# Where the decay exponents of a Mamba-2 scan are formed: matrix products before, broadcast rows with a Relu per head after

## The chip, the cores and the metric

The kernel runs on one core of a Trainium2 chip. The metric is device time in microseconds (us), the median of three runs of the whole kernel. Engines are named as in the profile: PE (TensorE, with its weight loads as PEld), DVE (VectorE), ACT (ScalarE), POOL (GpSimd), SP (the queue that issues most DMAs).

## The reference, cut to what matters

The input is 16 sequences of 512 tokens with 256 features. Each is normalized, goes through a Mamba-2 block with 8 heads, is normalized and added, and goes through a feed-forward block with ternary weights. Around the change, this is computed for every sequence:

```python
zxbcdt = x @ in_proj_w.T                        # z, x|B|C, dt
xBC = silu(conv4(xBC) + conv_b)
dt = softplus(dt + dt_bias)
dA = exp(dt * A)                                # A = -exp(A_log), one per head
S = dA_t * S + xdt_t[..., None] * B_t           # the scan over tokens
y_t = einsum('bhpn,bn->bhp', S, C_t)
```

Both kernels run the scan in four chunks of 128 tokens. Inside a chunk the output needs, for every head h, source token s and target token t, the factor exp(cum[t,h] - cum[s,h]) for t at or after s, where cum is the running sum of dt*A in the chunk. These factors fill a tile `mt` of 128 x (8 heads x 128) per chunk.

## The kernel before, in words

The order of work on PE, DVE, ACT and POOL is written out by hand: generator functions (stages) emit instructions, and `interleave` steps each stage between two fractions of a stretch. Each engine then runs its own instructions strictly in that order. Only SP's order is left to the scheduler. After a start with sequences 0 and 1, a loop of 14 turns does two stretches per turn, for three sequences at once:

- First stretch: input projections, convolution and gate of the next sequence (`stage_a`, blocks "b" and "z"), output projection and norms of the previous one (`stage_c1`), and on POOL the products of C with decays (`stage_e`, L533).
- Second stretch: feed-forward of the previous sequence (`stage_c2`: eight hidden blocks with Gelu, L756 and L762, then four output blocks, L790), the scan of the current one (`stage_b2`), and softplus, running sums and exponentials of the next (`stage_a2`, `stage_b0`, `stage_b1`).

The names that matter below:

- A convolution block is a product `pm` (PE, L323), a scaled copy to `cv` (ACT, L328), three multiply-adds on `cv` (DVE, L330) and a Silu (ACT, L335) that runs one block later (`lag=1`). The sixth block's Silu, which gives C, is emitted by `stage_a6` in the next first stretch.
- `stage_c1` makes `po` (PE, L710, one per chunk, in a pool of two PSUM banks) and `att` (DVE, L716), which needs the factor `rms` from a power on POOL (L585); then norm statistics whose power is on POOL (L258, `rs_c`), the second stream (L696), and a normalized copy (ACT, L282) that PE turns (L736) and DVE splits (`rests`, L740).
- `stage_a2` is softplus on 128x32: a Silu (L416), a reciprocal, and a series of eight coefficients `ATANH`, then `a = dt*A` (L465).
- `sums_of` makes three small products of `a` into `pd` (L477, L478), copies them to `sums` (DVE) and `cum` (ACT, L483), splits `cum` into three bf16 parts (L486 to L489), and brings these by DRAM (`away`, L491) into row groups of `lhs_e` and `rhs_e` (L492, L495).
- `stage_b1`: for each chunk two bf16 products `pe` of `lhs_e` with `rhs_e` (PE, L549, 128x512 each). These two constant tiles also hold ones and a mask, so that `pe` is already cum[t]-cum[s], or a large negative number. ACT takes exp of each (L553).
- `stage_b2`, per chunk: transposes `px` (L593), `xdt` (DVE, L595), `pg` with C.B (L599) and a turned B (L600), its masking (L602), a copy `bT` (DVE, L606), `xend` (POOL, L608), `mt = min(mt,1)*pg` (DVE, L611), the chunk's state `pst` (PE, L628), the decayed former state (POOL, L633) and their sum (DVE, L636), the output `py` (PE, L644 and L651) and `y` (DVE, L657).

The Exp functions need another ACT table than the Silus and the Gelus, so that each turn has three table loads: before the Gelus, before the Exps (L507), and before the Silus (L335).

Of the kernel before, what the change touches and what calls it, by code (L numbers as in the profile page):

```python
# [52 lines left out]
ATANH = [1.0 / k for k in (17, 15, 13, 11, 9, 7, 5, 3)]  # L54
# [3 lines left out]
def mamba_ffn_kernel(  # L58
# [25 lines left out]
    big = ctx.enter_context(tc.tile_pool(name="big", bufs=4))  # L84
# [31 lines left out]

    rhs_e = const.tile([P, NC, NH, P], BF16)
    lhs_e = const.tile([P, NC, P], BF16)  # L120

    def exponent_constants():

        nc.gpsimd.affine_select(
            out=rhs_e[:, 0], in_=rhs_e[:, 0], compare_op=ALU.is_ge, fill=-1e30, base=126,
            pattern=[[0, NH], [1, P]], channel_multiplier=-2,
        )
        yield 1.0
        for j in range(3):
            nc.gpsimd.affine_select(  # L130
                out=rhs_e[:, 0], in_=rhs_e[:, 0], compare_op=ALU.not_equal, fill=-1.0, base=-j,
                pattern=[[-3, NH], [0, P]], channel_multiplier=1,
            )
            yield 1.0

        for j in range(2):
            nc.gpsimd.affine_select(
                out=lhs_e, in_=lhs_e, compare_op=ALU.not_equal, fill=1.0, base=126 - j,
                pattern=[[0, NC], [1, P]], channel_multiplier=-2,
            )  # L140
            yield 1.0
        nc.gpsimd.memset(lhs_e[0:27], 1.0)
        for c in range(1, NC):
            nc.scalar.copy(rhs_e[:, c], rhs_e[:, 0])
            yield 1.0

# [293 lines left out]
    def stage_a2(b):  # L440


        W = NC * NH
        dt, neg, sil = seqs[b]["dt"], seqs[b].pop("neg"), seqs[b].pop("sil")
        df = dt.rearrange("p c h -> p (c h)")
        z = small.tile([P, W], F32, tag="sp_z", name=f"sp_z_{b}", bufs=1)
        nc.vector.scalar_tensor_tensor(z, neg, 2.0, sil, ALU.mult, ALU.subtract)
        nc.vector.reciprocal(z, z)
        nc.vector.tensor_mul(z, z, sil)
        e = small.tile([P, W], F32, tag="sp_e", name=f"sp_e_{b}", bufs=1)  # L450
        nc.vector.tensor_mul(e, z, z)
# [6 lines left out]
        for k in ATANH[4:]:  # L458
# [8 lines left out]
        sums_of(b, a)  # L467
        yield 0.3

    def sums_of(b, a):  # L470


        W = NC * NH
        af = a.rearrange("p c h -> p (c h)")
        pd = ps_tr.tile([P, 512], F32, tag="tr", name=f"pd_{b}")
        for i, tri in enumerate((after, ones)):
            nc.tensor.matmul(pd[:, i * W : (i + 1) * W], tri, af, start=True, stop=True)  # L477
        nc.tensor.matmul(pd[0:W, 2 * W : 2 * W + P], af, incl, start=True, stop=True)  # L478
        sums = small.tile([P, 2, W], F32, tag="sums", name=f"sums_{b}")
        nc.vector.tensor_copy(sums.rearrange("p i w -> p (i w)"), pd[:, 0 : 2 * W])  # L480
# [4 lines left out]
        rest = small.tile([W, P], F32, tag="cr", name=f"cr_{b}", bufs=1)  # L485
        nc.vector.tensor_copy(cp[:, 0, :], pc)  # L486
        nc.vector.tensor_sub(rest, pc, cp[:, 0, :])
        nc.vector.tensor_copy(cp[:, 1, :], rest)
        nc.vector.tensor_sub(cp[:, 2, :], rest, cp[:, 1, :])  # L489
        away = dram.tile([NC, NH, 3, P], BF16, tag="away", name=f"away_{b}")  # L490
        nc.sync.dma_start(away.rearrange("c h j t -> (c h) j t"), cp)  # L491
        nc.sync.dma_start(  # L492
            lhs_e[0:24], away.rearrange("c h j t -> (h j) c t")
        )
        nc.sync.dma_start(  # L495
            rhs_e[24:27].rearrange("j c h t -> j (c h) t"),
            away.rearrange("c h j t -> j (c h) t"),
        )
        seqs[b].update(sums=sums, cum=cum)


    def stage_b0(b):


        s = seqs[b]
        s["dec"] = small.tile([P, 2, NC, NH], F32, tag="dec", name=f"dec_{b}")
        nc.scalar.activation(  # L507
            s["dec"].rearrange("p i c h -> p (i c h)"), s["sums"].rearrange("p i w -> p (i w)"),
            AF.Exp,
        )  # L510
        cum = s.pop("cum")
        nc.scalar.activation(cum, cum, AF.Exp)
        s["way"] = dram.tile([NC * NH, P], F32, tag="way", name=f"way_{b}")
        nc.sync.dma_start(s["way"], cum)
        yield 0.1
# [24 lines left out]
    def stage_b1(b, lo, hi):  # L540

        mts = seqs[b].setdefault("mts", [])
        for c in range(lo, hi):
            n = f"{b}_{c}"
            mt = big.tile([P, NH, P], F32, tag="mt", name=f"mt_{n}")
            for q in range(2):
                hs = slice(4 * q, 4 * q + 4)
                pe = ps_a.tile([P, 512], F32, tag="a", name=f"pe_{n}_{q}")
                nc.tensor.matmul(  # L549
                    pe, lhs_e[:, c, :], rhs_e[:, c, hs, :].rearrange("p h t -> p (h t)"),  # L550
                    start=True, stop=True,
                )
                nc.scalar.activation(mt[:, hs, :].rearrange("p h t -> p (h t)"), pe, AF.Exp)  # L553
                yield 0.25
            mts.append(mt)


    def stage_b2(b):
# [28 lines left out]
        def prepare(c):  # L587
# [23 lines left out]
            nc.vector.scalar_tensor_tensor(  # L611
                mts[c], mts[c], 1.0, cbt.unsqueeze(1).to_broadcast([P, NH, P]), ALU.min, ALU.mult
# [8 lines left out]
        for c in range(NC):  # L621
# [3 lines left out]
            if c < NC - 1:  # L625
# [16 lines left out]
            for j in range(NJ):  # L642
# [7 lines left out]
                for h in (2 * j, 2 * j + 1):  # L650
# [3 lines left out]
                    )  # L654
            y = sb.tile([P, NJ, P], F32, tag="yt", name=f"y_{n}")
# [181 lines left out]
    A0_WORK, T0_WORK, A_WORK, A2_WORK, B1_WORK, B2_WORK = 1.0, 0.9, 18.1, 1.0, 0.5, 14.9  # L837
# [15 lines left out]
    with tc.manual_schedule(engines=ordered):  # L853
        nc.vector.memset(rhs_e[:, 0], 0.0)
        nc.vector.memset(lhs_e, 0.0)
# [29 lines left out]
        for i in range(1, NB - 1):  # L885
# [17 lines left out]
            second.append((stage_a2(i + 1), A2_WORK, 0.15, 0.5))  # L903
# [5 lines left out]
            interleave(*second)  # L909
        run(stage_a6(NB - 1))  # L910
# [52 lines left out]
```

## Time and profile before

| | |
|---|---|
| median of three runs (lowest to highest) | 1172.53 us (1172.21 to 1173.19) |
| the profiled execution | 1170.62 us, its span 1168.9 us |
| busy: PE, DVE, ACT, POOL | 1110.5 (95%), 850.3 (73%), 568.5 (49%), 594.6 us (51%) |
| mean granted PE clock | 0.98 |
| one turn of the loop | 68.50 us (ACT's first L553 of two successive turns starts at 578.02 and 646.52 us) |
| L549, the exponents' products | 128 on PE, 47.0 us busy |
| L553, their exponentials | 128 on ACT, 73.5 us busy, mean 595 ns |

How to read the rows that follow. A row of groups gives line, engine, operation, tiles written and read, shapes and count, then busy time and the mean of one, then how long the engine had been idle just before, and what ended that. A row of the timeline gives start and length in us, and in brackets how long the engine sat idle before it and which instruction ended the wait. Matmuls overlap in the pipeline: a row says 0.38 us for one, and what one costs in a full stream is the distance between starts.

### The profile page before, as it was taken

Reading aid. Unit: us, or ns where it says so; the run is one execution under the profiler, and the core shown is the slowest. Engines: PE = TensorE matmul, PEld = TensorE weight load, DVE = VectorE, ACT = ScalarE, POOL = GpSimd, SP = SyncE. Lnnn points to the kernel's source line nnn. Section 1 sums busy time; section 2 is a strip of 40 time slices with the busy share of each in tenths; the row PEclk is TensorE's granted clock in tenths of the full one; section 3 lists DMA queues with packets and bytes.
Section 4 is the critical chain, followed back from the end, with each engine's and each line's share of the span. In section 5 each row is a group of like instructions: output and inputs, shape, how many; then the busy total and the mean of one; then the engine's idle time right before and its main releaser. Section 6 shows DMA issues by size and latency. Waiting matters only on the chain.

```text
span 1168.9 us, 16958 instructions
## 1 busy us (share of the span) xinstructions
PE 1110.5 (95%) x6164; PEld 726.3 (62%) x6164; DVE 850.3 (73%) x2211; ACT 568.5 (49%) x957; POOL 594.6 (51%) x706
## 2 busy tenths in 40 slices
PE   5778899999999999999999999999999999999797
PEld 2335476675757667575765757576575756657475
DVE  4587977768687776868777686977768697786552
ACT  4725545446453544646355464635546463553321
POOL 3453545455454645546454554645455464555743
PEclk9888999999999999999999999999999999999899
DMA  5101011020100102010020101002020100201000
GB/s 194 40 19 57 19 43 52 4 73 19 68 27 31 64 5 72 19 67 28 20 74 4 73 19 67 27 10 85 4 72 19 68 27 4 72 5 72 2 10 27
DMA packets 28627, 48.57 MB, mean 42 GB/s; under 512 B 6656, under 2 KB 25728, under 8 KB 26496
## 3 DMA queue, kind: packets, MB, share of 16 engines
q1 hardware_dynamic: 26992, 47.33, 11.9%
q8 instruction: 48, 0.79, 0.3%
q10 hardware_dynamic: 1552, 0.16, 0.1%
q14 instruction: 35, 0.29, 0.1%
HBM read 38.44 MB, written 9.04 MB: 41 GB/s over the span
## 4 chain that ended last, share of the span: by engine, by line
PE 82%; DVE 7%; POOL 6%; ACT 3%; DMA 1%; issue 1%; POOLq 0%; ACTq 0%
PE pf L790 20%; PE pm L323 13%; PE ph L756 12%; PE po L710 9%; PE pz L345 8%; PE py L644 5%; PE pst L628 3%; PE py L651 3%; POOL x3p L744 3%; PE pe L549 2%; DVE cv L330 1%; POOL xend L608 1%; PE pt_a L300 1%; PE px L593 1%; PE pt_f L736 1%
## 5 line engine op out<-in xcount | busy, mean ns | idle before, releaser
L330 DVE SCALAR_TENSOR_TENSOR cv<-pm,cw_sb,cv 128x511 f32<-128x511 f32 (+2 forms) x288 | 215.3, 747 | 46.3 <-ACT cv L328 38.4
L790 PE MATMUL pf<-w_sb,hT 128*128 128x256 f32 x1024 | 248.8, 383 | 0.0
L790 PEld LDWEIGHTS pf<-w_sb,hT 128*128 128x128 f32 x1024 | 189.9, 190 | 42.3 <-issue 14.3
L756 PE MATMUL ph<-x3p,w_bf 128*128 128x512 bf16 x768 | 189.5, 382 | 2.3 <-ACT hT L762 0.4
L323 PE MATMUL pm<-x1T,win_sb 128*128 128x512 f32 x384 | 186.0, 607 | 0.0
L661 POOL TENSOR_TENSOR zs<-y,zs 128x512 f32<-128x512 f32 x64 | 81.7, 1277 | 204.2 <-DVE y L657 204.2
L762 ACT ACTIVATE hT<-ph,b_sb 128x512 f32<-128x512 f32 x128 | 88.0, 688 | 133.4 <-PE ph L756 133.2
L756 PEld LDWEIGHTS <-w_bf 128*128 128x128 bf16 x768 | 73.1, 98 | 92.7 <-issue 28.3
L553 ACT ACTIVATE mt<-pe 128x512 f32<-128x512 f32 x128 | 73.5, 595 | 110.3 <-PE pe L549 110.3
L328 ACT ACTIVATE cv<-pm,cw_sb 128x512 f32<-128x512 f32 x96 | 65.7, 684 | 120.7 <-PE pm L323 119.0
L345 PE MATMUL pz<-x1T,win_sb 128*128 128x512 f32 x256 | 124.0, 608 | 0.3 <-DVE dt L368 0.3
L710 PE MATMUL po<-wo_sb,zs 128*128 128x256 f32 x512 | 123.5, 385 | 0.3 <-DVE att L716 0.3
L323 PEld LDWEIGHTS pm<-x1T,win_sb 128*128 128x128 f32 x384 | 71.6, 194 | 72.7 <-issue 66.6
L533 POOL TENSOR_TENSOR ct<-ct,xbc 128x1024 f32<-128x1024 f32 x48 | 113.4, 2376 | 0.0
L710 PEld LDWEIGHTS po<-wo_sb,zs 128*128 128x128 f32 x512 | 94.7, 190 | 27.6 <-issue 16.6
L657 DVE SCALAR_TENSOR_TENSOR y<-xbc,dsk,py 128x128 f32<-128x128 f32 x256 | 71.2, 340 | 35.1 <-PE py L651 18.3
L644 PE MATMUL py<-mt,xdt 128*64 128x128 f32 x1024 | 95.7, 282 | 0.0
L796 DVE TENSOR_TENSOR o<-pf,b_sb 128x256 f32<-128x256 f32 x64 | 26.9, 420 | 86.7 <-PE pf L790 86.7
L349 ACT ACTIVATE zs<-pz 128x512 f32<-128x512 f32 x64 | 37.9, 592 | 93.4 <-PE pz L345 93.4
L345 PEld LDWEIGHTS pz<-x1T,win_sb 128*128 128x128 f32 x256 | 48.0, 194 | 55.9 <-issue 46.6
L611 DVE SCALAR_TENSOR_TENSOR mt<-mt,pg 128x1024 f32<-128x1024 f32 x64 | 77.6, 1212 | 0.5
L644 PEld LDWEIGHTS py<-mt,xdt 128*64 128x64 f32 x1024 | 60.3, 138 | 27.5 <-issue 12.9
(138 smaller groups left out, 1811.6 us busy)
## 6 DMA issues: line engine op xcount, KB each, us to landing
ct<-way SPq DMA_DIRECT2D x16, 1536.0 KB
xin<-in_x SPq DMA_DIRECT2D x16, 512.0 KB, 8.6
out<-o SPq DMA_DIRECT2D x30, 256.0 KB, 2.2
w_in<-in_w SPq DMA_DIRECT2D x1, 1024.0 KB
w_sb<-in_w SPq DMA_DIRECT2D x1, 1024.0 KB
win_sb<-in_w_in SPq DMA_DIRECT2D x1, 768.0 KB, 6.1
win_sb<-in_w_in SPq DMA_DIRECT2D x1, 512.0 KB
wo_sb<-in_w_out SPq DMA_DIRECT2D x1, 512.0 KB
```

Source lines behind the costliest of these rows:

```text
L323: nc.tensor.matmul(pm, win_sb[:, k, DI + m * P : DI + (m + 1) * P], x1T[:, k, :], start=(k == 0), stop=(k == 1),)
L330: nc.vector.scalar_tensor_tensor(cv[:, j:], pm[:, 0 : L - j], cw_sb[:, m, 3 - j : 4 - j], cv[:, j:], ALU.mult, ALU.add,)
L345: nc.tensor.matmul(pz, win_sb[:, k, j * P : (j + 1) * P], x1T[:, k, :], start=(k == 0), stop=(k == 1),)
L533: nc.gpsimd.tensor_tensor(ct[:, c - 1], ct[:, c - 1], xbc[:, 5, c * P : (c + 1) * P].unsqueeze(1).to_broadcast([P, NH, P]), ALU.mult,)
L553: nc.scalar.activation(mt[:, hs, :].rearrange("p h t -> p (h t)"), pe, AF.Exp)
L611: nc.vector.scalar_tensor_tensor(mts[c], mts[c], 1.0, cbt.unsqueeze(1).to_broadcast([P, NH, P]), ALU.min, ALU.mult)
L644: nc.tensor.matmul(py[h % 2 * HD : (h % 2 + 1) * HD, j, :], xdt[:, h * HD : (h + 1) * HD], mts[c][:, h, :], start=True, stop=(c == 0),)
L661: nc.gpsimd.tensor_tensor(zs[:, :, tok], y, zs[:, :, tok], ALU.mult)
L710: nc.tensor.matmul(po[:, 0:DM], g[:, k, c * P : (c + 1) * P], wo_sb[:, k, :], start=(k == 0), stop=(k == NJ - 1),)
L756: nc.tensor.matmul(ph, w1_bf[:, k, f * P : (f + 1) * P], x3p[:, j, k, :], start=(j == 0 and k == 0), stop=(j == 2 and k == 1),)
L762: nc.scalar.activation(hT[:, f, :], ph, AF.Gelu, bias=b1_sb[:, f : f + 1])
L790: nc.tensor.matmul(pf[:, 0:DM], hT[:, f, c * P : (c + 1) * P], w2_sb[:, f, :], start=(f == 0), stop=(f == NF - 1),)
```

## The change

The two constant tiles, their set-up (`exponent_constants`), the bf16 split, and the products `pe` go. The rows of `cum` are written to DRAM (`raw`) as float32, and a DMA per chunk brings the chunk's eight rows to all 128 partitions, straight into `mt` (`stage_r`). PE turns `cum` once per sequence, so that cum[s,h] stands as a column per head. ACT then forms max(0, cum[s]-cum[t]) in place, one Relu per head with that column as bias (`stage_s`, 32 per sequence), and one Exp with scale -1 per chunk (`stage_b1`). DVE's `min(...,1)` is no longer needed. The pool of `mt` has five tiles in place of four.

Also changed: the series has five coefficients; `bT` is copied by ACT; the decay of the state (POOL) is emitted right after the former state is known; the Silus of the loop's `stage_a` run two blocks late; `stage_e` starts at 0.18 of the first stretch and not at 0.06; `stage_a2` is at 0.08 to 0.36 of the second stretch and not at 0.15 to 0.5. Three of the four chunks get their Relus and Exps in the second stretch, the fourth at the head of the next first stretch.

```diff
-        for k in ATANH[1:4]:
+        for k in ATANH[1:3]:
...
-        cp = small.tile([W, 3, P], BF16, tag="cp", name=f"cp_{b}", bufs=1)
...
-        nc.sync.dma_start(
-            lhs_e[0:24], away.rearrange("c h j t -> (h j) c t")
-        )
...
+        raw = dram.tile([W, P], F32, tag="raw", name=f"raw_{b}")
+        nc.sync.dma_start(raw, cum)
+        seqs[b].update(sums=sums, cum=cum, raw=raw)
+        yield 0.15
+        turned = pd[:, 2 * W + P : 3 * W + P]
+        nc.tensor.transpose(turned, cum, ident[0:W, 0:W])
+        cums = small.tile([P, W], F32, tag="cums", name=f"cums_{b}", bufs=2)
+        nc.vector.tensor_copy(cums, turned)
...
-                nc.tensor.matmul(
-                    pe, lhs_e[:, c, :], rhs_e[:, c, hs, :].rearrange("p h t -> p (h t)"),
-                    start=True, stop=True,
-                )
-                nc.scalar.activation(mt[:, hs, :].rearrange("p h t -> p (h t)"), pe, AF.Exp)
...
+    def stage_r(b, *chunks):
+
+        mts = seqs[b].setdefault("mts", [])
+        for c in chunks:
+            mt = big.tile([P, NH, P], F32, tag="mt", name=f"mt_{b}_{c}")
+            nc.sync.dma_start(
+                mt.rearrange("p h t -> p (h t)"),
+                seqs[b]["raw"][c * NH : (c + 1) * NH, :].rearrange("h t -> (h t)")
+                .partition_broadcast(P),
+            )
...
+    def stage_s(b, *chunks):
...
+            for h in range(NH):
+                nc.scalar.activation(
+                    mt[:, h, :], mt[:, h, :], AF.Relu,
+                    bias=s["cums"][:, c * NH + h : c * NH + h + 1], scale=-1.0,
+                )
...
+    def stage_b1(b, *chunks):
...
+            nc.scalar.activation(mt, mt, AF.Exp, scale=-1.0)
...
-                nc.vector.tensor_copy(bT, pg[:, P : 2 * P])
+                nc.scalar.copy(bT, pg[:, P : 2 * P])
...
-            nc.vector.scalar_tensor_tensor(
-                mts[c], mts[c], 1.0, cbt.unsqueeze(1).to_broadcast([P, NH, P]), ALU.min, ALU.mult
+            nc.vector.tensor_tensor(
+                mts[c], mts[c], cbt.unsqueeze(1).to_broadcast([P, NH, P]), ALU.mult
...
-                (stage_a(i + 1, BESIDE), A_WORK - 1.72, 0.0, 1.0),
+                (stage_a(i + 1, BESIDE, 2), A_WORK - 1.72, 0.0, 1.0),
+                (chain(stage_s(i, 3), stage_b1(i, 3)), 1.1, 0.0, 0.01),
                 (stage_c1(i - 1), C1_WORK, 0.0, 1.0),
-                (stage_e(i), E_WORK, 0.06, 1.0),
+                (stage_e(i), E_WORK, 0.18, 1.0),
...
-                (stage_b1(i + 1, 0, 2), 2 * B1_WORK, 0.68, 0.8),
...
+                (stage_r(i + 1, 0, 1), 0.2, 0.365, 0.37),
+                (stage_s(i + 1, 0), 1.0, 0.44, 0.49),
...
+                (stage_s(i + 1, 2), 1.0, 0.72, 0.8),
+                (stage_b1(i + 1, 2), 0.1, 0.81, 0.82),
+                (stage_r(i + 1, 3), 0.1, 0.82, 0.83),
```

With this, the orders that the compiled programs have around the head of the first stretch are, on ACT: before `cv` of block 0, a square (L572), table load, Silu of block 5, `cv` of block 1; after `cv` of block 0, two Relus, the square, six Relus, Exp, table load, Silu of block 5, `cv` of block 1. On POOL: before the first C product, `rs_c`, `off_c`, `rms`; after `rs_c`, `off_c`, the first C product, `rms`. DVE's order there is the same in both: `cv` of block 0, `att` of chunk 0, `cv` of block 1, `att` of chunks 1, 2 and 3.

More of the change, by code (lines that the diff above doesn't have):

```diff
@@ L51 @@
 EPS = 1e-5
-ATANH = [1.0 / k for k in (17, 15, 13, 11, 9, 7, 5, 3)]
+ATANH = [
+    0.12144778747160243, 0.10715370454912052, 0.14308298362334984, 0.1999944417776,
+    0.333333377501784,
+]
 @with_exitstack
@@ L83, in mamba_ffn_kernel @@
     one = ctx.enter_context(tc.tile_pool(name="one", bufs=1))
[L84 removed]
+    big = ctx.enter_context(tc.tile_pool(name="big", bufs=5))
     sb = ctx.enter_context(tc.tile_pool(name="sb", bufs=2))
@@ L115, in mamba_ffn_kernel @@
     )
[L119 to L126, printed above, removed]
-        )
[L128 to L132, printed above, removed]
-            )
[L134 to L145, printed above, removed]
     mhalf = const.tile([P, NC], F32)
@@ L454, in stage_a2 @@
         nc.vector.tensor_scalar_mul(acc, e, ATANH[0])
-        for k in ATANH[1:4]:
+        for k in ATANH[1:3]:
             nc.vector.scalar_tensor_tensor(acc, acc, k, e, ALU.add, ALU.mult)
         yield 0.15
-        for k in ATANH[4:]:
+        for k in ATANH[3:]:
             nc.vector.scalar_tensor_tensor(acc, acc, k, e, ALU.add, ALU.mult)
@@ L466, in stage_a2 @@
         yield 0.25
-        sums_of(b, a)
-        yield 0.3
+        yield from sums_of(b, a)
     def sums_of(b, a):
@@ L483, in sums_of @@
         nc.scalar.copy(cum, pc)
-        cp = small.tile([W, 3, P], BF16, tag="cp", name=f"cp_{b}", bufs=1)
[L485 to L491, printed above, removed]
-        nc.sync.dma_start(
-            lhs_e[0:24], away.rearrange("c h j t -> (h j) c t")
[L494 to L499, printed above, removed]
+        raw = dram.tile([W, P], F32, tag="raw", name=f"raw_{b}")
[6 more added lines that the diff above has]
+        nc.vector.tensor_copy(cums, turned)
+        seqs[b].update(cums=cums)
+        yield 0.15
     def stage_b0(b):
@@ L510, in stage_b0 @@
         )
-        cum = s.pop("cum")
-        nc.scalar.activation(cum, cum, AF.Exp)
+        ecum = small.tile([NC * NH, P], F32, tag="ecum", name=f"ecum_{b}", bufs=1)
+        nc.scalar.activation(ecum, s.pop("cum"), AF.Exp)
         s["way"] = dram.tile([NC * NH, P], F32, tag="way", name=f"way_{b}")
-        nc.sync.dma_start(s["way"], cum)
+        nc.sync.dma_start(s["way"], ecum)
         yield 0.1
@@ L537, in stage_e @@
             yield 0.7 if c == 1 else 0.15
-    def stage_b1(b, lo, hi):
+    def stage_r(b, *chunks):
         mts = seqs[b].setdefault("mts", [])
[L543 to L549, printed above, removed]
-                    pe, lhs_e[:, c, :], rhs_e[:, c, hs, :].rearrange("p h t -> p (h t)"),
-                    start=True, stop=True,
-                )
-                nc.scalar.activation(mt[:, hs, :].rearrange("p h t -> p (h t)"), pe, AF.Exp)
-                yield 0.25
-            mts.append(mt)
+        for c in chunks:
[5 more added lines that the diff above has]
+            )
+            mts.append(mt)
+            yield 0.1
+    def stage_s(b, *chunks):
+        s = seqs[b]
+        for c in chunks:
+            mt = s["mts"][c]
+            for h in range(NH):
+                nc.scalar.activation(
+                    mt[:, h, :], mt[:, h, :], AF.Relu,
+                    bias=s["cums"][:, c * NH + h : c * NH + h + 1], scale=-1.0,
+                )
+                if h % 2 == 1:
+                    yield 0.25
+    def stage_b1(b, *chunks):
+        for c in chunks:
+            mt = seqs[b]["mts"][c]
+            nc.scalar.activation(mt, mt, AF.Exp, scale=-1.0)
+            yield 0.1
     def stage_b2(b):
@@ L628, in stage_b2 @@
                 nc.tensor.matmul(pst, bT, xend, start=True, stop=True)
-                nstate = sb.tile([P, DI], F32, tag="state", name=f"state_{n}")
                 if c == 0:
+                    nstate = sb.tile([P, DI], F32, tag="state", name=f"state_{n}")
                     nc.scalar.copy(nstate, pst)
                 else:
-                    nc.gpsimd.tensor_tensor(
-                        heads(nstate), heads(state), over_d(dec[:, 1, c, :]), ALU.mult
-                    )
+                    nstate = decayed
                     nc.vector.tensor_tensor(nstate, pst, nstate, ALU.add)
@@ L654, in stage_b2 @@
                     )
+            if c + 1 < NC - 1:
+                decayed = sb.tile([P, DI], F32, tag="state", name=f"state_{b}_{c + 1}")
+                nc.gpsimd.tensor_tensor(
+                    heads(decayed), heads(nstate), over_d(dec[:, 1, c + 1, :]), ALU.mult
+                )
             y = sb.tile([P, NJ, P], F32, tag="yt", name=f"y_{n}")
@@ L836, in mamba_ffn_kernel @@
     E_WORK = 1.0
-    A0_WORK, T0_WORK, A_WORK, A2_WORK, B1_WORK, B2_WORK = 1.0, 0.9, 18.1, 1.0, 0.5, 14.9
+    A0_WORK, T0_WORK, A_WORK, A2_WORK, B2_WORK = 1.0, 0.9, 18.1, 1.0, 14.9
     C1_WORK, C2_WORK = 1.0, 24.2
@@ L853, in mamba_ffn_kernel @@
     with tc.manual_schedule(engines=ordered):
-        nc.vector.memset(rhs_e[:, 0], 0.0)
-        nc.vector.memset(lhs_e, 0.0)
         interleave(
@@ L860, in mamba_ffn_kernel @@
             ),
-            (exponent_constants(), 9.0, 0.1, 0.5),
             (stage_a0(1), A0_WORK, 0.04, 0.28),
             (chain(stage_sil(0), stage_a2(0)), 0.1 + A2_WORK, 0.42, 0.85),
+            (stage_r(0, 0, 1, 2, 3), 0.4, 0.86, 0.87),
+            (stage_s(0, 0, 1), 2.0, 0.9, 1.0),
             (scales(), 6.0, 0.55, 1.0),
@@ L869, in mamba_ffn_kernel @@
             (stage_a(1, SECOND), A_WORK, 0.0, 0.8),
+            (stage_s(0, 2, 3), 2.0, 0.0, 0.11),
             (stage_b0(0), 0.1, 0.11, 0.111),
             (stage_d(0), 0.1, 0.111, 0.112),
-            (stage_b1(0, 0, NC), 4 * B1_WORK, 0.112, 0.1121),
+            (stage_b1(0, 0, 1, 2, 3), 0.4, 0.112, 0.1121),
             (stage_b2(0), B2_WORK, 0.2, 0.9),
@@ L878, in mamba_ffn_kernel @@
             (stage_a6(1), 0.1, 0.86, 0.861),
+            (stage_r(1, 0, 1, 2), 0.3, 0.755, 0.765),
+            (stage_r(1, 3), 0.1, 0.85, 0.86),
+            (stage_s(1, 0, 1), 2.0, 0.8, 0.87),
             (stage_b0(1), 0.1, 0.88, 0.881),
-            (stage_b1(1, 0, 2), 2 * B1_WORK, 0.89, 0.9),
-            (stage_b1(1, 2, 4), 2 * B1_WORK, 0.94, 0.98),
+            (stage_b1(1, 0, 1), 0.2, 0.89, 0.9),
+            (stage_s(1, 2), 1.0, 0.9, 0.94),
+            (stage_b1(1, 2), 0.1, 0.95, 0.96),
             (stage_d(1), 0.1, 0.95, 0.96),
@@ L895, in mamba_ffn_kernel @@
             second = [
+                (stage_r(i + 1, 0, 1), 0.2, 0.365, 0.37),
+                (stage_s(i + 1, 0), 1.0, 0.44, 0.49),
                 (stage_b0(i + 1), 0.1, 0.5, 0.51),
-                (stage_b1(i + 1, 0, 2), 2 * B1_WORK, 0.68, 0.8),
-                (stage_b1(i + 1, 2, 3), B1_WORK, 0.86, 0.9),
-                (stage_b1(i + 1, 3, 4), B1_WORK, 0.95, 0.99),
+                (stage_b1(i + 1, 0), 0.1, 0.515, 0.52),
+                (stage_s(i + 1, 1), 1.0, 0.53, 0.61),
+                (stage_b1(i + 1, 1), 0.1, 0.62, 0.63),
+                (stage_r(i + 1, 2), 0.1, 0.63, 0.64),
+                (stage_s(i + 1, 2), 1.0, 0.72, 0.8),
+                (stage_b1(i + 1, 2), 0.1, 0.81, 0.82),
+                (stage_r(i + 1, 3), 0.1, 0.82, 0.83),
             ]
@@ L902, in mamba_ffn_kernel @@
             second.append((stage_b2(i), B2_WORK, 0.0, 0.98))
-            second.append((stage_a2(i + 1), A2_WORK, 0.15, 0.5))
+            second.append((stage_a2(i + 1), A2_WORK, 0.08, 0.36))
             second.append((stage_a5(i + 1), 1.7, 0.58, 0.66))
@@ L909, in mamba_ffn_kernel @@
             interleave(*second)
+        run(stage_s(NB - 1, 3))
+        run(stage_b1(NB - 1, 3))
         run(stage_a6(NB - 1))
```

## The prediction

> **What bounds the kernel now.** I read the chain of work that ended last, then one turn of the loop in the timelines of PE, DVE, ACT and POOL, each beside the compiled order of both kernels. The chain:
>
> ```profile
> PE 82%; DVE 7%; POOL 6%; ACT 3%; DMA 1%; issue 1%; POOLq 0%; ACTq 0%
> ```
>
> PE carries it. In a turn (590.66, the start of the first convolution product, to 659.15 us) PE's timeline shows one wait, 0.40 us before `pst`; everything else runs start to start. So a product taken out is worth its distance to the next start, not its busy time:
>
> ```profile
> 646.10 0.38 PE L549 MATMUL pe<-rhs_e,lhs_e 128*128 128x512 bf16 x1
> 646.32 1.03 PE L790 MATMUL pf<-w_sb,hT 128*128 128x256 f32 x4
> ```
>
> That is 0.22 us, though the mean of L549 is 0.39. But in the first stretch PE is not alone. DVE's timeline there:
>
> ```profile
> 593.39 2.31 DVE L330 SCALAR_TENSOR_TENSOR cv<-pm,cw_sb,cv 128x511 f32<-128x511 f32 x3
> 595.61 0.47 DVE L716 SCALAR_TENSOR_TENSOR att<-po,rms,x 128x256 f32<-128x256 f32 x1
> ...
> 596.82 2.32 DVE L330 SCALAR_TENSOR_TENSOR cv<-pm,cw_sb,cv 128x511 f32<-128x511 f32 x3
> 599.05 0.47 DVE L716 SCALAR_TENSOR_TENSOR att<-po,rms,x 128x256 f32<-128x256 f32 x1
> ...
> 602.35 0.48 DVE L716 SCALAR_TENSOR_TENSOR att<-po,rms,x 128x256 f32<-128x256 f32 x1 [0.68 <-PE pqt L367]
> ...
> 608.39 0.18 DVE L368 TENSOR_TENSOR dt<-pqt,dtb 128x32 f32<-128x32 f32 x1
> ...
> 616.93 0.68 DVE L595 TENSOR_TENSOR xdt<-px,dt 128x512 f32<-128x512 f32 x1
> ```
>
> From 593.39 to 616.93 the only bracket is 0.68 us: DVE is full as well, and after that it has 12.1 us of brackets up to 658.55 (1.25, 0.22, 1.53, 0.21, 0.32, 0.66, 1.61, 1.19, 1.87, 3.25). Hence the rule for the sum: work taken off DVE in the second stretch is worth nothing, and any wait put on DVE in the first counts nearly in full, for `rests` (L740), then POOL's `x3p`, `xend` and PE's `pst` follow it. ACT and POOL at the same place:
>
> ```profile
> 592.66 0.69 ACT L328 ACTIVATE cv<-pm,cw_sb 128x512 f32<-128x512 f32 x1 [1.79 <-PE pm L323]
> 593.24 0.62 ACT L572 ACTIVATE y<-zs 128x512 f32<-128x512 f32 x1
> 593.88 1.28 ACT L335 ACT_TABLE_LOAD   x1
> 595.18 0.72 ACT L335 ACTIVATE xbc<-cv,cb_sb 128x512 f32<-128x512 f32 x1
> 596.10 0.69 ACT L328 ACTIVATE cv<-pm,cw_sb 128x512 f32<-128x512 f32 x1 [0.20 <-PE pm L323]
> ```
>
> ```profile
> 596.00 2.38 POOL L533 TENSOR_TENSOR ct<-ct,xbc 128x1024 f32<-128x1024 f32 x1
> 600.49 0.70 POOL L258 TENSOR_TENSOR rs_c<-rs_c,mhalf 128x2 f32<-128x2 f32 x1 [2.11 <-DVE rs_c L257]
> 601.27 0.20 POOL L271 TENSOR_TENSOR off_c<-mv_c,rs_c 128x2 f32<-128x2 f32 x1
> 601.42 0.56 POOL L585 TENSOR_TENSOR rms<-rms,mhalf 128x1 f32<-128x1 f32 x1
> ```
>
> The `cv` of block 1 comes on ACT just when PE has the product ready. POOL does the first C product in idle time, before `rs_c`.
>
> **What comes off PE.** Eight products a turn at 0.21 to 0.31, together 1.83; one turn of `cum` comes on, near the 0.11 of one of the four `px` products (0.43 for four). Net 1.7 us a turn.
>
> **What comes off DVE.** Per sequence the four split rows (L486 to L489, 1.05 us), three steps of the series (0.35 to 0.53 each, 1.3) and three `bT` copies (0.9), less one copy of `cums` (0.2). All lie in the second stretch, under its 12.1 us of waits: nothing. The early state decay ends DVE's wait for POOL (28.7 us over 16 sequences, all there too): nothing. If that cover were gone they would be worth up to 4 us a turn. The `mt` product stays at 1.2 us, 1024 columns either way.
>
> **The transfers.** Three issues of 24 KB go, a 16 KB write and four of 512 KB come, 33.5 MB in all. SP runs in order: the fetch of chunk 2 waits for `py` of chunk 1, that of chunk 3 for `py` of chunk 2, and behind them stand `way`, the C decays (`ct`), the outputs and the next input. The C decays need the end of `py` of chunk 3 anyway, and land early enough: in the windows of 2 us their 1.5 MB take about 5 us after issue at 650.62, and POOL wants them at 664. A fetch of a third of that is 2 us plus the 1.4 that `way` takes to land; chunk 0 has some 6 us between `cum` and its first Relu. Taken as nothing; late by 2 us would be at most 2 us a turn, since PE's `pf` products and the buffers then cover part. Nothing below zero.
>
> **The Relus on ACT, and the wait they make.** No row shows one. The nearest: L512, 128 columns without a bias column, 292 ns; a bias column adds 93 (L762 688 against L553 595, both 512 from PSUM); neighbours overlap by 0.10 (four L282 of 0.59 take 2.06). So 0.29 us apart, eight take 2.3. With neither the column's price nor the overlap right they would be 0.2 to 0.4, 1.6 to 3.2. An Exp of 1024 columns is 595 + 512 x 0.854 = 1.03 us (slope from L512 and L572). In the second stretch ACT gets three such chunks after the last Gelu, about 16 us of work with x1 and the copies before the next turn, in some 21 us: covered. In the first stretch the fourth chunk is queued between `cv` of block 0 and `cv` of block 1: 2.3 + 1.03 - 0.1 = 3.25 us more. ACT was free for `cv` of block 1 at 595.81, so now at 599.06, 2.96 late. DVE is then at exactly this instruction with nothing to do, and `att` of chunks 1 to 3 are queued behind it. PE's fourth `po` (600.26) needs the bank that `att` of chunk 1 frees (599.52): it stalls about 2.3 us.
>
> Here the skill speaks against the change: "ScalarE: Activation LUTs", Rules for kernel authors, puts relu on VectorE. The rows give no gain an element: DVE's 128x128 takes 290 ns (L602). But by that rule this chunk would put 2.3 us of work on DVE and leave only the Exp on ACT; the turn would be some 0.7 us shorter than with a 3.0 us wait, 1211 in place of 1220.
>
> **The step moved on POOL.** The first C product (2.38) now stands between `off_c` and `rms`. `rs_c` follows the late `cv`, 600.49 + 2.96 = 603.45; `off_c` ends at 604.4, the C product at 606.8, `rms` at 607.3. DVE's `att` of chunk 3 needs that `rms`: 607.35 in place of 602.35, 5.0 us late. Behind it stand 14.6 us of full DVE up to `xdt`, with `dt`, whose reading frees a bank for PE's third `pz`: a second stall, near 2.3. The whole turn moves by 5.0.
>
> **The sum.** A turn: +5.0 - 1.7 = +3.3. In the first turn the Silu of block 5 is ahead of the burst, with no table load in it: +1.3. The start loses 16 products (-3.5) but has 16 Relus (4.6) before the copies of x1T that PE waits for, and the way by DRAM before those: +3 (-4 to +8). The end has no `cv`, only the last burst of 3.3 us in front of a Silu and a C product: +1 (0 to 3). Together 13 x 3.3 + 1.3 + 3 + 1 = 48. The profiled execution of 1170.62 us (span 1168.9) becomes 1218.6; the median stands 1.9 above it: 1220.
>
> **The clock.** The windows grant 1.00 from 160 to 1090 us. Early on, after a short wait:
>
> ```profile
> 53.14 2.52 PE L549 MATMUL pe<-rhs_e,lhs_e 128*128 128x512 bf16 x5 [2.17 <-ACT cum L512]
> ```
>
> Five take 2.52, where 4 x 0.22 + 0.38 = 1.26 is usual, and the next `pz` takes 3.78 and not 1.88: half speed, some 3.2 us lost. "TensorE: Matmul & The Clock Gate", Part 1, wants an idle window of about 3.4 us before the clock is halved; by that the two stalls of 2.3 cost no more. By the row they do; then the first loss of 3.2 eats the second stall of 2.3, +0.9 a turn, and one after the second stall up to +1.7 more likely hidden behind DVE. Main case zero; with it +13 to +24.
>
> **The rivals.**
> 1. The burst hides, and the products taken off PE are simply gained: 14 x 1.7 + 3.5 = 27, 1145 us. For it: 82% of the chain is PE, ACT is at 49%. It decides if `cv` of block 1 comes by about 596.8, that is, if 3.25 us of burst cost DVE less than 0.7; the rows leave no room for that unless DVE's fullness is itself stretched by waiting on PE. Chance 0.19.
> 2. The burst stalls DVE, but the C product on POOL doesn't hold `rms`: 2.3 - 1.7 = +0.6 a turn, about 1186. For it: POOL has 2 us of idle before `rs_c`; against it, POOL's order is fixed. Chance 0.14.
> 3. As forecast, and the clock falls in the stalls: 1233 to 1244. Chance 0.13.
> The forecast, 1205 to 1228, has 0.54.
>
> A measurement of this kernel can tell about 0.2% (2.3 us) from no change. Range 1174 to 1244: it leaves out rival 1 and little else. Faster 0.19, same 0.02, slower 0.79.
>
> **What would show it.** Turn length 71.8 against 68.50; no L549, PE starts otherwise as close as before; a bracket of 3 us on DVE before `cv` of block 1, ended by ACT; one on `att` ended by POOL `rms`, 2 us or more; PE waits on DVE `att` and `dt`. Wrong if DVE's first stretch has brackets below 1 us, if Relus stand 0.2 us apart, or if PE waits for `mt` or a DMA.

## The result and the profile after

| | before | after |
|---|---|---|
| median (lowest to highest) | 1172.37 us (1169.49 to 1173.19, 4 runs) | 1260.86 us (1259.64 to 1263.13, 4 runs) |
| ratio, 95% interval | | 1.0762 (1.0737 to 1.0786) |
| profiled execution, span | 1168.9 us | 1261.4 us |
| busy PE, DVE, ACT, POOL | 95, 73, 49, 51% | 88, 65, 56, 47% |
| mean granted PE clock | 0.980 | 0.962 |
| mean turn | 68.50 us | 75.01 us |

The change costs 7.6%, where 4.1% was forecast (1220, range 1174 to 1244). "Mean turn" here and below is the mean of the twelve distances between PE's first `pt_f` of sequences 1 to 13, read off PE's timeline. By the same rows the span's 92.5 us fall as follows: 8.7 before the first `pt_f`, 7.0 in the first distance, 78.2 in these twelve, 3.7 and -5.0 in the last two, nothing behind them. (The medians differ by 88.5; the profiled execution is the longest of the four.) So it is the loop, and not the ends.

The chain of the changed kernel, against 82% of PE before:

```profile
PE 56%; ACT 17%; DVE 16%; POOL 6%; issue 3%; DMA 1%; SPq 0%; ACTq 0%; POOLq 0%
```

The end is no longer set by PE alone; a third of the way runs through ACT and DVE. Where, is seen in one turn (its block 0 is at 641.99 us, where the rows of before start at 593.39). DVE's timeline:

```profile
641.99 2.31 DVE L302 SCALAR_TENSOR_TENSOR cv<-pm,cw_sb,cv 128x511 f32<-128x511 f32 x3
...
648.32 2.31 DVE L302 SCALAR_TENSOR_TENSOR cv<-pm,cw_sb,cv 128x511 f32<-128x511 f32 x3 [2.94 <-ACT cv L300]
...
655.81 0.48 DVE L701 SCALAR_TENSOR_TENSOR att<-po,rms,x 128x256 f32<-128x256 f32 x1 [2.77 <-POOL rms L566]
...
661.84 0.18 DVE L340 TENSOR_TENSOR dt<-pqt,dtb 128x32 f32<-128x32 f32 x1
...
670.37 0.68 DVE L576 TENSOR_TENSOR xdt<-px,dt 128x512 f32<-128x512 f32 x1
```

Both brackets that the forecast named are here: 2.94 before `cv` of block 1 (2.96 forecast), and 2.77 before `att` of chunk 3, for POOL's `rms`. From block 0 to `xdt` it is 28.38 us, against 23.54 before: 4.84 more, where 5.0 was forecast. ACT and POOL beside it:

```profile
641.06 0.69 ACT L300 ACTIVATE cv<-pm,cw_sb 128x512 f32<-128x512 f32 x1 [2.62 <-PE pm L295]
...
642.75 1.85 ACT L524 ACTIVATE mt<-mt,cums 128x128 f32<-128x128 f32 x6
644.63 1.06 ACT L535 ACTIVATE mt<-mt 128x1024 f32<-128x1024 f32 x1
...
646.99 0.72 ACT L307 ACTIVATE xbc<-cv,cb_sb 128x512 f32<-128x512 f32 x1
647.62 0.67 ACT L300 ACTIVATE cv<-pm,cw_sb 128x512 f32<-128x512 f32 x1
```

```profile
651.98 0.70 POOL L230 TENSOR_TENSOR rs_c<-rs_c,mhalf 128x2 f32<-128x2 f32 x1 [7.32 <-DVE rms L565]
...
652.91 2.34 POOL L498 TENSOR_TENSOR ct<-ct,xbc 128x1024 f32<-128x1024 f32 x1
655.22 0.56 POOL L566 TENSOR_TENSOR rms<-rms,mhalf 128x1 f32<-128x1 f32 x1
```

The second `cv` of ACT has no bracket: its product was there, and ACT came to it late. POOL sat idle for 7.32 us, and after `rs_c` and `off_c` it took the C product ahead of the short power (`rms`) that DVE wanted. PE's two stalls follow, 2.27 and 2.03 (2.3 and 2.3 forecast):

```profile
651.08 1.99 PE L695 MATMUL po<-wo_sb,zs 128*128 128x256 f32 x8 [2.27 <-DVE att L701]
...
662.08 1.98 PE L317 MATMUL pz<-x1T,win_sb 128*128 128x512 f32 x4 [2.03 <-DVE dt L340]
```

What the forecast doesn't have is a third stall in the second stretch. From the list of waits (us in total, times, longest):

```profile
ACT bT L587 <- DVE pg L583: 65.1, 33, 15.2
...
PE ph L741 <- ACT hT L747: 23.9, 15, 2.4
```

And in the timelines of ACT and PE:

```profile
674.25 0.27 ACT L587 COPY bT<-pg 128x128 f32<-128x128 f32 x1 [2.10 <-DVE pg L583]
...
675.82 0.69 ACT L747 ACTIVATE hT<-ph,b_sb 128x512 f32<-128x512 f32 x1
```

```profile
676.56 1.83 PE L741 MATMUL ph<-x3p,w_bf 128*128 128x512 bf16 x6 [2.08 <-ACT hT L747]
678.32 1.98 PE L623 MATMUL py<-mt,xdt 128*64 128x128 f32 x16
```

`bT` is half of the tile `pg`, whose other half DVE masks; the copy waits for that mask, which stands in DVE's queue. The first Gelu stands behind the copy on ACT, and PE's third hidden block waits for that Gelu's tile. The two rows of PE also run slowly: such a `py` group of 16 takes 1.09 us in the turn before. This turn is not the usual one: in ten of thirteen turns the stall at `ph` is 1.45 to 1.70 us, and the slow rows come earlier, after the stall at `pz`. In the windows the loop of before had a clock of 1.00. The row of the changed kernel ends with the clock, the DMA share and GB/s:

```profile
160.00:640.00 480.00, 441.62 (x2458) 291.78 (x2477) 320.54 (x818) 283.82 (x585) 227.03 (x269) 0.98 0.20 69
```

### The profile page after: what moved, and what is told of

It reads as the page before. It is cut to its first block, busy times and chain, and to the rows that moved or that the text cites. A ratio compares the mean times of both kernels' runs of the same rounds, so it can differ in the third digit from the quotient of the medians.

```text
span 1261.4 us, 17181 instructions
## 1 busy us (share of the span) xinstructions
PE 1112.0 (88%) x6007; PEld 724.8 (57%) x6052; DVE 820.3 (65%) x2065; ACT 712.0 (56%) x1450; POOL 588.9 (47%) x699
## 4 chain that ended last, share of the span: by engine, by line
PE 56%; ACT 17%; DVE 16%; POOL 6%; issue 3%; DMA 1%; SPq 0%; ACTq 0%; POOLq 0%
PE pf L775 18%; PE ph L741 11%; PE pm L295 7%; PE py L623 5%; DVE cv L302 5%; PE pz L317 4%; ACT mt L524 4%; PE py L630 3%; POOL ct L498 3%; ACT xbc L307 2%; DVE st_f L223 2%; PE pst L609 2%; ACT cv L300 2%; DVE x L681 2%; ACT mt L535 2%
## 5 line engine op out<-in xcount | busy, mean ns | idle before, releaser
L775 PE MATMUL pf<-w_sb,hT 128*128 128x256 f32 x1024 | 238.0, 382 | 0.0
L295 PE MATMUL pm<-x1T,win_sb 128*128 128x512 f32 x384 | 190.5, 620 | 12.8 <-ACT x1T L275 12.8
L524 ACT ACTIVATE mt<-mt,cums 128x128 f32<-128x128 f32 x512 | 161.0, 388 | 2.6 <-DVE cv L302 1.8
L317 PE MATMUL pz<-x1T,win_sb 128*128 128x512 f32 x256 | 132.2, 642 | 26.5 <-DVE dt L340 26.5
L741 PEld LDWEIGHTS <-w_bf 128*128 128x128 bf16 x768 | 70.8, 98 | 114.1 <-issue 50.9
L554 POOL TENSOR_TENSOR y<-y 128x256 f32<-128x256 f32 x64 | 46.5, 727 | 129.9 <-ACT y L553 129.8
L592 DVE TENSOR_TENSOR mt<-mt,pg 128x1024 f32<-128x1024 f32 x64 | 78.2, 1221 | 30.3 <-ACT bT L587 29.7
L230 POOL TENSOR_TENSOR rs_c<-rs_c,mhalf 128x2 f32<-128x2 f32 x32 | 25.1, 785 | 131.1 <-DVE rms L565 95.2
```

The costliest lines, as they stand in the source:

```text
L295: nc.tensor.matmul(pm, win_sb[:, k, DI + m * P : DI + (m + 1) * P], x1T[:, k, :], start=(k == 0), stop=(k == 1),)
L317: nc.tensor.matmul(pz, win_sb[:, k, j * P : (j + 1) * P], x1T[:, k, :], start=(k == 0), stop=(k == 1),)
L524: nc.scalar.activation(mt[:, h, :], mt[:, h, :], AF.Relu, bias=s["cums"][:, c * NH + h : c * NH + h + 1], scale=-1.0,)
L741: nc.tensor.matmul(ph, w1_bf[:, k, f * P : (f + 1) * P], x3p[:, j, k, :], start=(j == 0 and k == 0), stop=(j == 2 and k == 1),)
L775: nc.tensor.matmul(pf[:, 0:DM], hT[:, f, c * P : (c + 1) * P], w2_sb[:, f, :], start=(f == 0), stop=(f == NF - 1),)
```

## The experiments

The theory after the result: three stalls in a turn, each from where one piece of work is placed (the burst ahead of `cv` of block 1, `stage_e` at 0.18, `bT` on ACT), with half a clock behind some of them; the exponents off PE are a gain. The rival: the Relus on ACT or the fetches cost the time by themselves. First each stall is taken out of the changed kernel, then each cause put alone into the kernel before, then each left alone.

### One stall taken out, then all three

`bT` by DVE again:

```diff
-                nc.scalar.copy(bT, pg[:, P : 2 * P])
+                nc.vector.tensor_copy(bT, pg[:, P : 2 * P])
```

> The changed kernel with one edit: bT is copied by DVE again, not by ACT. Theory: on ACT, the copies of bT wait for DVE's masking of pg (2.1 us in the changed kernel), the first Gelu stands behind them, and PE waits 2.08 us a turn for the bank that this Gelu frees. Without it: 14 x 2.1 = 29 us less, some 1232 us, PE's waits for hT near nothing, DVE's waits for bT gone. Rival: the Gelu is late because of the Silu that lag 2 leaves behind; then little changes, 1255 to 1262, and PE still waits for hT.

The C products at 0.06 again:

```diff
-                (stage_e(i), E_WORK, 0.18, 1.0),
+                (stage_e(i), E_WORK, 0.06, 1.0),
```

> The changed kernel with one edit: stage_e starts at 0.06 of the first stretch again, so that POOL does the first C product before rs_c. Theory: DVE's wait of 2.77 us a turn for POOL's rms goes, and PE's second stall (2.03 us, third pz, behind dt) with it; the wait of 2.9 us for cv stays: 14 x 2.4 = 34 us less, near 1227. Rival: the early product waits for the late Silu of block 5 and holds rs_c itself, so that the same wait returns one instruction earlier: no gain, 1255 or more.

The fourth chunk's burst moved to the end of the second stretch:

```diff
-                (chain(stage_s(i, 3), stage_b1(i, 3)), 1.1, 0.0, 0.01),
+                *([(chain(stage_s(1, 3), stage_b1(1, 3)), 1.1, 0.0, 0.01)] if i == 1 else []),
...
+                (stage_s(i + 1, 3), 1.0, 0.925, 0.938),
+                (stage_b1(i + 1, 3), 0.1, 0.985, 0.99),
...
-        run(stage_s(NB - 1, 3))
-        run(stage_b1(NB - 1, 3))
```

> The changed kernel with one edit: the Relus and the Exp of the fourth chunk are done at the end of the second stretch, around the copies of x1T, and not between cv of blocks 0 and 1. Theory: DVE's wait of 2.94 us for cv of block 1 goes, and PE's stall of 2.27 before the fourth po; POOL's C product still holds rms, by about 2 us: 14 x 2.7 = 38 us less, near 1222. Rival: the Relus in their new place delay the copies of x1T, so that PE waits for them by up to 2 us a turn; then 1240 to 1260.

All three edits together:

> All three edits together in the changed kernel. Theory: only these three waits, and the half-speed clock that they bring about (mean 0.98 in the loop, some 1.5 us a turn), cost time, and the products taken off PE are worth 1.7 us a turn: turn of 66.8 us against 75.08, with a start slower by some 8 us: 1150, 2% below the kernel before. Rival: the Relus load ACT so much that other waits take their place: 1172 or more.

Measured, beside 1171.48 for before:

| | us | ratio (interval) | mean turn | what is left of PE's stalls a turn |
|---|---|---|---|---|
| `bT` by DVE | 1224.71 | 1.0459 (1.0442 to 1.0477) | 72.5 | `po`, `pz` |
| C products early | 1221.06 | 1.0416 (1.0393 to 1.0439) | 71.7 | `po`, `ph` |
| burst moved | 1223.29 | 1.0445 (1.0426 to 1.0465) | 71.9 | `pz`, `ph` |
| all three | 1157.97 | 0.9886 (0.9872 to 0.9901) | 67.4 | none |

Each takes out its own stall, for 36, 40 and 38 us (29, 34 and 38 expected). Together they give 103 us, and the kernel is 1.1% faster than before with all 32 Relus and four Exps of a sequence still on ACT and all fetches in place. Ten of the twelve turns take 67.0 us, 1.5 less than before. So the rival falls, and the same move of the exponents is a gain in one order and a loss in another. The smaller edits that stay in all these versions (the shorter series, the early decay of the state, the Silus two blocks late) were not tested by themselves.

### One cause put alone into the kernel before

Each exponent product issued twice:

```diff
-                nc.tensor.matmul(
-                    pe, lhs_e[:, c, :], rhs_e[:, c, hs, :].rearrange("p h t -> p (h t)"),
-                    start=True, stop=True,
-                )
+                for _ in range(2):
+                    nc.tensor.matmul(
+                        pe, lhs_e[:, c, :], rhs_e[:, c, hs, :].rearrange("p h t -> p (h t)"),
+                        start=True, stop=True,
+                    )
```

> The kernel before, with each of its 128 exponent products (L549) issued twice into the same tile; the second computes the same again. This asks what such a product costs the turn, the other way round: 8 more in each turn. Theory (0.21 us for each, as the matmul records lie apart, and TensorE is the bound in these places): 128 x 0.21 = 27, so about 1199 us, turns of 70.2. Rival A (a product costs its mean busy time of 0.39): 50 us more, about 1222. Rival B (the products lie in gaps of TensorE, so that taking them away gave nothing): 1172 to 1177.

The C products late:

```diff
-                (stage_e(i), E_WORK, 0.06, 1.0),
+                (stage_e(i), E_WORK, 0.18, 1.0),
```

> The kernel before, with one constant of the change: the products with C (stage_e, GpSimd) begin at 0.18 of the first stretch, not at 0.06. Nothing else is changed, so TensorE still has its exponent products. Theory (a 2.3 us product then stands between two powers on GpSimd, the last att is late and TensorE waits about 2 us in each turn for po or pz): 13 turns x 2 = 26 at full clock, about 1198; if the wait also brings half a clock for a stretch, as taking it out of the changed kernel gave 40 us, about 1210. Rival (GpSimd's order only hurts behind the long ACT burst): 1172 to 1180, and the wait of att for rms stays short.

`bT` by ACT:

```diff
-                nc.vector.tensor_copy(bT, pg[:, P : 2 * P])
+                nc.scalar.copy(bT, pg[:, P : 2 * P])
```

> The kernel before, with one line of the change: the turned B (bT) is copied by ScalarE, not VectorE. Theory (ScalarE waits for VectorE's mask in the same tile, the Gelu queued behind it is late, TensorE waits about 2 us in each turn for hT): 13 x 2.1 = 27 at full clock, about 1200, or about 1208 with the slower clock that went with it in the changed kernel. Rival (with less on ScalarE in these places the copy waits but nothing behind it is late, and VectorE gains three copies a turn): 1168 to 1175, and no wait of TensorE for hT.

Measured, beside 1171.67 for before:

| | us | ratio (interval) | every turn |
|---|---|---|---|
| products twice | 1194.32 | 1.0201 (1.0186 to 1.0216) | 70.2 |
| C products late | 1194.41 | 1.0198 (1.0183 to 1.0213) | 70.1 |
| `bT` by ACT | 1191.81 | 1.0178 (1.0161 to 1.0195) | 69.8 |

Eight more products lengthen a turn by 1.7 us, 0.21 each: the distance of starts, not the mean busy time of 0.39, is the price. In all it is 22.7 us and not 27, for the first `pt_f` comes no later (125.94 against 127.72): in the start the products cost nothing. The two moves cost 1.6 and 1.3 us a turn, less than the 2 expected. The list of waits has them in the kernel before as in the changed one. Of the C products late:

```profile
DVE att L716 <- POOL rms L585: 37.2, 14, 2.8
PE pz L345 <- DVE dt L368: 20.1, 15, 1.9
```

Of `bT` by ACT:

```profile
ACT bT L606 <- DVE pg L602: 63.5, 34, 13.1
...
PE ph L756 <- ACT hT L762: 17.3, 15, 1.8
```

In both the windows grant 1.00 from 160 to 1040 us: these shorter stalls bring no half clock. Such a stall in the timeline of the C products late, with the usual 1.98 behind it:

```profile
763.58 1.98 PE L345 MATMUL pz<-x1T,win_sb 128*128 128x512 f32 x4 [1.37 <-DVE dt L368]
```

### One stall left in the changed kernel

Only the burst (the edits of the first two experiments):

> The changed kernel with two of the mends (bT by VectorE, the products with C at 0.06), so that of the three stalls only the burst of eight Relus and an Exp ahead of block 1's cv is left. Theory (one stall alone costs its own wait, 1.3 to 1.7 us of a turn at full clock, as the two others did in the kernel before; the rest of the changed kernel's loss comes where stalls follow each other and bring half a clock): turns of 68.5, about 1179 us, granted clock 1.00 between 160 and 640. Rival (each stall costs about 3 us of a turn by itself, as taking each out of the changed kernel gave): turns of 70.1, about 1200, clock below 1.00.

Only the late C products (`stage_e` at 0.18 in the version with all three):

> The version with all three mends, with one of them undone: the products with C begin at 0.18 again, so of the three stalls only the late power of GpSimd is left. In the kernel before the same constant cost 1.6 us of a turn. Theory (the same here, since the clock stays whole with one stall): turns of 68.6, about 1181. Rival (behind the schedule of the change it costs the 3.2 that taking it out of the changed kernel gave): turns of 70.2, about 1201.

Measured, beside 1170.99: burst alone 1201.86, 1.0264 (1.0246 to 1.0281), mean turn 70.8; C products alone 1187.23, 1.0141 (1.0123 to 1.0159), turns of 69.2 to 69.4 but for one of 72.4.

The second lies between: 2.2 us a turn, not 1.6 and not 3.2, at a clock of 1.00 but for the turn of 72.4. The first speaks against the theory that one stall leaves the clock whole: its windows grant 0.98, and its turns come in two kinds. Its PE timeline in two successive turns:

```profile
618.63 2.42 PE L695 MATMUL po<-wo_sb,zs 128*128 128x256 f32 x8 [2.29 <-DVE att L701]
...
621.06 3.08 PE L317 MATMUL pz<-x1T,win_sb 128*128 128x512 f32 x4
...
689.74 1.99 PE L695 MATMUL po<-wo_sb,zs 128*128 128x256 f32 x8 [2.30 <-DVE att L701]
691.68 1.88 PE L317 MATMUL pz<-x1T,win_sb 128*128 128x512 f32 x4
```

The wait is the same. Behind it the rows are slow in one turn and at full speed in the next. Of thirteen such waits of 2.29 or 2.30 nine are followed by slow rows and four are not; turns of 69.4 belong to the latter, turns of 71.1 to 71.6 to the former. So the clock is lost by one stall of this length, not by several in a row, and it is worth 1.7 to 2.2 us when it happens.

Why one and not the other is seen in the granted clock, which changes in this trace only at the bounds of stretches of 3.41 us that follow one another. (A row gives bounds, length, then the busy time of PE, PEld, DVE, ACT and POOL, the granted clock, the DMA share and GB/s.)

```profile
616.65:620.06 3.41, 1.43 (x7) 1.28 (x8) 3.23 (x9) 0.00 (x0) 1.56 (x2) 1.00 0.00 0
620.06:623.47 3.41, 3.41 (x7) 1.73 (x6) 2.63 (x9) 0.00 (x0) 1.76 (x4) 0.50 0.00 0
...
688.33:691.74 3.41, 2.00 (x10) 1.75 (x11) 3.16 (x10) 0.00 (x0) 1.48 (x4) 1.00 0.00 0
691.74:695.15 3.41, 3.41 (x10) 1.50 (x10) 2.77 (x9) 0.60 (x1) 1.73 (x3) 1.00 0.00 0
```

Of the first wait 1.98 us lie in one stretch, PE is busy for only 1.43 us of it, and the next stretch has half the clock. The second wait is split by a bound at 688.33; PE is busy for 2.52 us of the stretch before that bound and 2.00 of the one behind it, and the clock stays.

### The start and the last turns

The version with all three mends has its first `pt_f` 4.7 us later than before (132.45 against 127.72). Its first sequence's Relus were moved:

```diff
-            (stage_s(0, 0, 1), 2.0, 0.9, 1.0),
...
-            (stage_s(0, 2, 3), 2.0, 0.0, 0.11),
+            (stage_s(0, 0), 1.0, 0.02, 0.1),
...
-            (stage_b1(0, 0, 1, 2, 3), 0.4, 0.112, 0.1121),
+            (stage_b1(0, 0), 0.1, 0.112, 0.1121),
+            (stage_s(0, 1), 1.0, 0.13, 0.18),
+            (stage_b1(0, 1), 0.1, 0.185, 0.19),
+            (stage_s(0, 2), 1.0, 0.24, 0.3),
+            (stage_b1(0, 2), 0.1, 0.31, 0.32),
+            (stage_s(0, 3), 1.0, 0.4, 0.47),
+            (stage_b1(0, 3), 0.1, 0.48, 0.49),
```

A first form of this had the later chunks at 0.13 to 0.54, so that the third chunk of the first sequence was multiplied by the masked C.B product before its Exp (the product starts at 64.30 us, the Exp at 65.54): it leaves the exponential out of that product. It took 1148.35 us. What was expected of this first form:

> The version with all three mends, and its start mended: the first sequence's 32 Relus no longer come 16 ahead of the second sequence's turned copies (x1T) and 16 in one burst behind them, but 8 for each chunk ahead of its Exp, spread over the second part of the start. Theory (the start is 8.4 us late against the kernel before because TensorE waits 7.7 for x1T and VectorE 13 for ScalarE's cv there): 6 to 8 us less, 1150 to 1152. Rival (the Relus are then late for the first chunk products and the same time is lost there): within 2 us of 1158.

And of the form above:

> The version with all three mends and its start mended: the first sequence's Relus no longer 16 ahead of the second sequence's turned copies (x1T) and 16 in one burst behind them, but 8 for each chunk, all behind those copies, each chunk's 8 ahead of its Exp and of its product with the masked B. Theory (TensorE's 7.7 us wait for x1T at the start goes): dec of the third sequence at 157 in place of 165, in all 8 to 10 us less than with three mends, 1148 to 1150. Rival (the Relus are then late for the first chunk products, and the time is lost there): within 2 us of 1158.

Measured with the form above: 1148.04 us beside 1170.99, 0.9803 (0.9788 to 0.9819). The size is as expected, the reason is not: the 7.7 us wait for `x1T` is still there, at 98.45 us. What went is an earlier wait for `x1T` of 4.42 us at 47.27. Half clock went too: to 70 us the windows now grant 1.00, where they granted 0.90; but of the three half-clock stretches there (from 17.22, 34.29 and 44.53 us) only the last lies at that wait, and what took away the others was not looked into.

In these versions some of the last turns take longer (here 68.5 to 70.6, where the others take 67.0 or 67.1). It is seen in the timelines of ACT and PE:

```profile
962.24 2.46 ACT L524 ACTIVATE mt<-mt,cums 128x128 f32<-128x128 f32 x8 [2.04 <-DMA mt<-raw]
```

```profile
983.65 0.83 PE L561 MATMUL pss<-ones,sq 128*128 128x1 f32 x6 [1.96 <-ACT x1T L275]
```

The Relus wait for their rows, because the 16 KB write of `raw` lands after up to 3.5 us where 1.4 is usual, and some 20 us later PE waits for the turned copies that stand behind them on ACT. So the Relus were given room:

```diff
-                (stage_s(i + 1, 0), 1.0, 0.44, 0.49),
-                (stage_b0(i + 1), 0.1, 0.5, 0.51),
-                (stage_b1(i + 1, 0), 0.1, 0.515, 0.52),
+                (stage_b0(i + 1), 0.1, 0.44, 0.45),
+                (stage_s(i + 1, 0), 1.0, 0.475, 0.515),
+                (stage_b1(i + 1, 0), 0.1, 0.52, 0.525),
```

> The version with three mends and the mended start, with one move: in the second stretch the Exps of the decays (dec, ecum) stand ahead of the first chunk's eight Relus, not behind them, and the Relus come a little later. In the version without it the last four turns take 68.5 to 70.9 in place of 67.0, and in just these ScalarE waits 1.3 to 2.0 us at these Relus for their rows (mt from raw), because the 16 KB write of raw lands after 3.3 us and not 1.4. Theory (that wait, by way of the turned copies x1T, is what makes these turns longer; with 2 us more of room it is hidden): 67.0 in all 13 turns, and 1148 less 8, about 1140 us. Rival (the turns are longer for something else that the wait only shows): the wait goes, the turns stay, 1146 to 1149; or the later Relus make every turn longer, over 1150.

Measured: 1146.11 us (1143.46 to 1147.14) beside 1170.25, 0.9797 (0.9780 to 0.9813). All twelve turns of the profiled execution now take 67.2, and ACT no longer waits at these Relus, though the write still lands late at times (3.4 at most): so there the wait was what made the turns longer. But by the medians the kernel is only some 2 us faster than the version without the move, not 8, and the two intervals overlap. The profiled execution without the move was the slowest of its four (1149.65), the one with it the fastest (1143.46); how long the turns of the others were is not on record. This is the fastest version, 2.0% faster than before, and its chain is PE's again:

```profile
PE 81%; DVE 6%; ACT 5%; POOL 5%; DMA 1%; issue 1%; POOLq 0%; ACTq 0%; DVEq 0%
```

## Why the prediction was wrong

The direction and the two named stalls were right; two terms set at nothing, `bT` on ACT and the clock, were not nothing, and with them the time left the range.

- **What comes off PE, 1.7 a turn: right.** 1.7 by the doubled products, 1.5 by the version without stalls (67.0 against 68.5).
- **The burst, 2.96 late: right.** 2.94 in the trace. Six Relus of 0.39 take 1.85, so they are 0.29 apart, as estimated, the Exp takes 1.06, where 1.03 was forecast.
- **The C product ahead of `rms`: right.** `att` of chunk 3 waits 2.77; DVE's first stretch is 4.84 longer, 5.0 forecast. PE's stalls are 2.27 and 2.03.
- **The turn of 71.8: right for what it counted.** The version without stalls, 67.0, with the burst at full clock (69.4, +2.4) and the C products (69.2, +2.2) makes 71.6.
- **`bT`: the first failed term.** The forecast put it among "What comes off DVE", three copies for 0.9 us, under DVE's waits: nothing. It priced what the copy leaves and not where it arrives: three copies on ACT, each behind a wait for DVE, with Gelus behind them. That waiting instruction is the kind of thing the forecast looked for in the first stretch and not in the second. Alone it costs 1.3 us a turn. Beside one of the other stalls, in turns at full clock, it costs 2.2 (71.65 with the burst, against 69.4 for the burst alone) or 1.7 (70.9 with the C products, against 69.2); taken out of the changed kernel 2.5.
- **The clock: the second failed term.** "Main case zero" took the rule's 3.4 us window over the row of 2.17 that stood beside it. The row was right, and rival 3 had the mechanism and the size: of the turn of 75.0, 71.6 and the 1.7 to 2.2 of `bT` leave 1.2 to 1.7 for the clock, worked out from these runs rather than measured by itself; rival 3 had 0.9 to 1.7. The trace agrees: between 200 and 1120 us it has thirteen half-clock stretches of 3.41 us, one a turn, and each can hold PE back by at most 1.7. With the burst moved, turns with such a stretch take 72.5 and those without 70.9.
- **The start, +3: too small, 8.7.** The end, +1, is -5.0 in the last distance.

Together: forecast 44.2 for the fourteen turns, measured 88.8 (7.0 + 78.2 + 3.7); the miss of 44.6 is 3.2 a turn, and `bT` and the clock are 3.4 by the figures above (75.0 less 71.6). That the misses at start and end, 5.7 and -6.0, nearly cancel is luck.

**The rivals.** Rival 1 (1145) is wrong for this kernel, and yet near to what the change is worth once the three placements are undone: 1158, and 1146 with the start mended. Rival 2 falls with the 2.77 us for `rms`. Moving the Relus to DVE, as the rule on relu has it, was not tried: with the burst elsewhere ACT has room for them.

## What to carry to other kernels

Where each engine runs a fixed order, price an operation that moves to another engine at its new place: what it waits for there, and what stands behind it; three copies of 0.27 us cost 1.3 to 2.5 us a turn, because they waited for a masking in another engine's queue and Gelus stood behind them. (That they wait because copy and masking use two halves of one tile is read from the kernel; no run gave `bT` a tile of its own.) A change that seems bad may be a good one in a bad order: put each of its parts alone into the old kernel before giving it up. And when a row of the same trace disagrees with a rule, let the main case follow the row.

## What the runs showed of the hardware that was not expected

- **Half a clock when PE is busy for less than about 1.5 of 3.41 us.** "TensorE: Matmul & The Clock Gate", Part 1, halves the clock after an idle window of about 3.4 us and says that this window runs freely, so that the same kernel can fall differently into it. The traces agree with the second and not with the first. From 160 to 1040 us of all fourteen traces the clock changes only at the bounds of stretches of 3.41 us. With the products of one column (`pss`) left out, PE was busy for 1.00 to 1.46 us of each of the 41 stretches behind which the clock was halved. Of the 3527 full-speed stretches behind which it wasn't, PE was busy for 1.48 us or more in all but one, which has 1.40. (The ends of matmul records are modelled, so the last digits are rough.) The forecast's own row fits: before it, PE is busy for 1.04 us from 49.94 to 53.36, and the clock is 0.50 from there.
- **So a wait counts by where it falls.** Thirteen waits of 1.15 to 1.17 and twenty-six of 1.37 to 1.63 in the loops (the two kernels in which only the C products are late, and the kernel before with `bT` by ACT) were followed by full speed each time: by the figures above a stretch has to hold about 1.95 us of idle time (3.41 less 1.46). Waits of 2.03 to 2.30 do or don't, by where a bound splits them. Products of one column hardly count as work: in the first form of the mended start, 1.27 us of waiting and six of them (0.83) lie in one stretch (910.36 to 913.77), and the next `pm` group takes 3.57 in place of 1.96; in the second form a wait of 1.96 with the same six behind it is split at 982.57, and the group takes 1.96.
- **A 16 KB write to DRAM that lands late in some turns.** 1.4 us in nearly all turns; in every version made from the changed kernel one to four of the last turns (issued from 815 us on) have 3.0 to 3.7, and the changed kernel itself has none above 1.4. What it shares its path with there stays open.
